# Quantized feed-forward stages: one float8 cast per block of 512 tokens in place of three

## The chip, the cores and the metric

The kernel runs on one core of one Trainium2 chip. The metric is the device time of one execution in microseconds (us); lower is better. A core has five instruction queues that matter here: TensorE (PE, matrix products, its weight loads shown apart as PEld), VectorE (DVE), ScalarE (ACT), GpSimd (POOL) and SyncE (SP, which issues the transfers).[...]

## The reference, cut to what matters

The network has four layers. The change touches the two quantized feed-forward nets in it, one in layer 2 (called f2 in the kernel) and one in layer 3 (f3). Both compute the same thing on 16,384 tokens of 96 channels, with a hidden width of 384:

```python
q_mul = lambda x: _float_quantize(x, 5, 2)     # float8, 5 exponent bits, 2 mantissa bits
q_acc = lambda x: _float_quantize(x, 5, 10)    # float16

def _qlinear(x, W, b):
    y = q_acc(jnp.einsum('bsk,nk->bsn', q_mul(x), q_mul(W)))
    return q_acc(y + q_mul(b))

h = jax.nn.relu(_qlinear(x, W1, b1))
y = _qlinear(h, W2, b2)
...
t = t + _L3_ffn_ref(_ln_t(t), L3_ffn_W1, L3_ffn_b1, L3_ffn_W2, L3_ffn_b2)
```

So each hidden value is a matrix product rounded to float16, plus a bias and again rounded to float16, cut at zero, and then rounded to float8 because it enters the second product through q_mul.

## The kernel before, in words

The token stream is kept on the chip as t, 96 channels on the partitions by 16,384 tokens, and is worked in blocks of 512 tokens (MB). A feed-forward net therefore has 32 blocks. One block goes through these steps, with the lines that the profile names:

- `center` (L881 on PE, L883 on ACT): subtract the channel mean by a product with a centring matrix, and square the result.
- `scale` (L887 on PE, L889 and L890 on ACT): sum the squares with a matrix of ones and form the reciprocal root.
- `norm` (L893 on DVE): multiply the two, and write the normed block as float8, the tile xq.
- `hidden`: three times over (m = 0, 1, 2, one third of the 384 hidden channels each) a float8 product on PE into a bank of its own (L1033), a copy to float16 on ACT (L1035, tile y), bias and cut at zero on DVE from float16 to float16 (L1037, tile y2), and a cast to float8 on POOL into a third of the tile hq (L1038).
- `project`: three products of hq with the second weights into one bank (L1044 on PE), a copy to float16 on DVE (L1046, tile z), the bias on DVE (L1048, tile z2), and the sum into t on POOL (L1050). In f3 a transfer to the output follows (L1053).

The order on every queue is the order in which the program issues the steps: the stages are built under `tc.manual_schedule`, so nothing is reordered. In `qffn` (the f3 net) iteration j of the loop issues `scale(j-1)`, `center(j)`, `norm(j-2)`, `project(j-5)`, `hidden(j-3)`. From that follows, for each queue and one iteration:

- PE: two sums of squares, two centrings, three L1044 of block j-5, three L1033 of block j-3.
- ACT: L889, L890, L883, then three L1035.
- DVE: L893 (xq), L1046 (z), L1048 (z2), then three L1037 (y2).
- POOL: one L1050 (t), then three L1038 (hq).

In `layer2` the f2 net runs with the same steps in the same order, after an attention part. Its first blocks share the loop with the last blocks of that attention: there an L978 product on PE and an L980 sum into t on DVE stand ahead of `project`, and L978 uses the same bank as L1044 (tag "o", one buffer). After those the f2 net runs alone with the norms of the next stage. Everything after f2 (the Fourier stage) starts from what f2 leaves in t, and f3 is the last stage of the kernel.

Tiles come from pools with a fixed number of buffers: y and y2 have four of 128x512 each, hq three of 128x3x512, z and z2 two, each bank of L1033 one. A writer waits until the last reader of the buffer is done. The profile drops trailing digits of names, so both y and y2 appear as y, both z and z2 as z.

Of the kernel before, what the change touches and what calls it, by code (L numbers as in the profile page):

```python
# [10 lines left out]
F16 = mybir.dt.float16  # L11
# [3 lines left out]
ALU = mybir.AluOpType  # L15
# [7 lines left out]
MB = 512  # L23
# [27 lines left out]
class Net:  # L51
# [967 lines left out]
    def ffn_steps(self, k, t, wk, psum, tags, out=None):  # L1019
        nc = self.nc  # L1020
        w1, w2, b1, b2 = self.ffn[k]
        x, hq = {}, {}

        def xq(i):
            x[i] = wk.tile([C, MB], F8, name="xq", tag="xq", bufs=2)
            return x[i]

        def hidden(i):
            xi = x.pop(i)
            q = hq[i] = wk.tile([128, 3, MB], F8, name="hq", tag="hq", bufs=3)  # L1030
            for m in range(3):
                ps = psum.tile([128, MB], F32, name="h_ps", tag=tags[m])
                nc.tensor.matmul(ps, w1[:, m * 128 : (m + 1) * 128], xi, start=True, stop=True)  # L1033
                y = wk.tile([128, MB], F16, name="y", tag="y", bufs=4)
                nc.scalar.copy(y, ps)  # L1035
                y2 = wk.tile([128, MB], F16, name="y2", tag="y2", bufs=4)
                nc.vector.tensor_scalar(y2, y, b1[:, m : m + 1], 0.0, ALU.add, ALU.max)  # L1037
                nc.gpsimd.tensor_copy(q[:, m, :], y2, saturate=False)  # L1038

        def project(i):  # L1040
            ps = psum.tile([C, MB], F32, name="y_ps", tag=tags[3])
            q = hq.pop(i)
            for m in range(3):
                nc.tensor.matmul(ps, w2[:, m, :], q[:, m], start=m == 0, stop=m == 2)  # L1044
            z = wk.tile([C, MB], F16, name="z", tag="z", bufs=2)
            nc.vector.tensor_copy(z, ps)  # L1046
            z2 = wk.tile([C, MB], F16, name="z2", tag="z2", bufs=2)
            nc.vector.tensor_scalar_add(z2, z, b2)  # L1048
            td = t[:, i * MB : (i + 1) * MB]
            nc.gpsimd.tensor_add(td, td, z2)  # L1050
            if out is not None:
                b, s = divmod(i, L // MB)
                nc.sync.dma_start(out[b, :, s * MB : (s + 1) * MB], td)  # L1053

        return hidden, project, xq

    def qffn(self, t, k, out):
# [397 lines left out]
```

## Time and profile before

| | |
|---|---|
| median of 3 runs | 4002.08 us (3991.09 to 4005.25) |
| the profiled execution | 4009.92 us |
| span of its trace, first to last instruction | 4007.8 us |
| busy in the span: PE, DVE, ACT, POOL | 3303.4, 3186.9, 2421.0, 2944.4 us |
| f2 net, first to last L1038 | from 3160.5 us, about 144 us |
| f3 net, last 125 us of the span | first L1046 at 3885.7 us, last L1038 at 4000.4 us |

Busy time is what an engine's instructions covered between their first and last moment, waiting inside an instruction included. A group line of the profile reads: line, engine, operation, output<-inputs, shape and type of output and input, count, then the busy time in us and the mean of one instruction in ns, then the idle time of the engine ahead of these instructions and what ended it. A line of the timeline reads: start in us from the span's beginning, length in us, engine, line, operation, names and shapes, how many equal instructions it joins, and in square brackets the idle time before it and what released it. Instructions on one engine overlap slightly in such lists[...].

### The profile page before, as it was taken

How to read it: one execution, taken by the hardware profiler on the slowest of the kernel's cores; microseconds unless marked ns; L12 is line 12 of the kernel's file. 1: busy time of each engine (PE TensorE's matmuls, PEld its weight loads, DVE VectorE, ACT ScalarE, POOL GpSimd, SP SyncE). 2: the span in 40 equal slices, each digit the busy share in tenths (PEclk: the TensorE clock that was granted, in tenths of full speed). 3: DMA queues.
4: the chain of work that ended last, by engine and by line, in shares of the span. 5: the costliest groups of instructions: out<-in, count | busy, mean ns of one | idle time of the engine just before them, and what ended most of it. 6: DMA issues, size and time to landing. Idle time of an engine off the chain costs nothing. (4 is left out here: it accounts for less than half of the span.)

```text
span 4007.8 us, 45514 instructions
## 1 busy us (share of the span) xinstructions
PE 3303.4 (82%) x14174; PEld 1425.1 (36%) x14174; DVE 3186.9 (80%) x2772; ACT 2421.0 (60%) x4644; POOL 2944.4 (73%) x1571
## 2 busy tenths in 40 slices
PE   6888878888888788888878888686999888998877
PEld 3222222222222222222222222186445435676642
DVE  5999999999999999999999999832652593444549
ACT  4666667667666766766666666231445575665547
POOL 2999999999999999999999999811000273444428
PEclk8888878878888888888888888667999998999989
DMA  7567566756666675666567666375000000011111
GB/s 184 137 161 174 135 160 157 175 131 168 166 154 148 162 170 138 162 166 167 141 161 169 147 155 158 82 226 178 1 0 1 1 0 6 25 35 35 42 41 54
DMA packets 183295, 468.13 MB, mean 117 GB/s; under 512 B 53240, under 2 KB 55170, under 8 KB 179972
## 3 DMA queue, kind: packets, MB, share of 16 engines
q1 hardware_dynamic: 183048, 465.21, 46.8%
q8 instruction: 113, 1.85, 0.2%
q14 instruction: 134, 1.07, 0.1%
HBM read 391.53 MB, written 73.50 MB: 116 GB/s over the span
## 5 line engine op out<-in xcount | busy, mean ns | idle before, releaser
L496 POOL TENSOR_TENSOR hs<-hs,crep 128x1024 f32<-128x1024 f32 x768 | 1796.2, 2363 | 27.2 <-DVE hs L490 22.4
L454 PE MATMUL rep<-dbl,sel_b 32*128 32x512 f32 x1152 | 409.0, 787 | 460.4 <-DVE hs L490 434.4
L474 POOL TENSOR_TENSOR up<-udb,brep 128x1024 f32<-128x1024 f32 x256 | 604.9, 2363 | 8.5 <-DMA brep<-cd 8.5
L468 ACT ACTIVATE da<-ddb,nega 128x1024 f32<-128x1024 f32 x512 | 584.9, 1149 | 14.9 <-DMA ddb<-dd 7.4
L468 ACT ACTIVATE dap<-ddb,nega 128x1024 f32<-128x1024 f32 x256 | 286.3, 1118 | 419.6 <-DVE hs L490 417.5
L515 PE MATMUL y<-hs,sel_r 128*32 128x512 f32 x3072 | 483.2, 697 | 6.1 <-POOL hs L496 6.1
L490 DVE TENSOR_TENSOR_SCAN hs<-da,state,rep 128x1024 f32<-128x1024 f32 x192 | 450.8, 2348 | 16.7
L490 DVE TENSOR_TENSOR_SCAN hs<-da,state,u 128x1024 f32<-128x1024 f32 x192 | 450.9, 2348 | 11.2 <-DVE u L486 1.4
L490 DVE TENSOR_TENSOR_SCAN hs<-dap,state,up 128x1024 f32<-128x1024 f32 x192 | 447.1, 2329 | 7.0 <-ACT dap L468 6.9
L454 PEld LDWEIGHTS rep<-dbl,sel_b 32*128 32x128 f32 x1152 | 109.6, 219 | 761.6 <-issue 510.0
L210 PE MATMUL ps<-n,w_x 97*64 97x512 f32 x1536 | 368.0, 622 | 8.1 <-ACT n L323 5.4
L486 DVE TENSOR_TENSOR u<-udb,rep 128x1024 f32<-128x1024 f32 x256 | 314.6, 1229 | 42.1 <-PE rep L454 10.9
L486 DVE TENSOR_TENSOR rep<-udb,rep 128x1024 f32<-128x1024 f32 x256 | 310.7, 1214 | 0.4
L1038 POOL CAST hq<-y 128x512 fp8e5<-128x512 f16 x192 | 118.0, 638 | 229.3 <-issue 143.0
L210 PEld LDWEIGHTS ps<-n,w_x 97*64 97x64 f32 x1536 | 109.8, 141 | 258.8 <-issue 209.2
L515 PEld LDWEIGHTS y<-hs,sel_r 128*32 128x32 f32 x3072 | 66.6, 117 | 364.5 <-issue 192.7
L382 POOL TENSOR_TENSOR du<-delta,xc 128x512 f32<-128x512 f32 x96 | 122.3, 1274 | 67.5 <-DMA gp_x<-in_x 52.1
L1177 POOL TENSOR_TENSOR av<-av,ec 128x780 f32<-128x780 f32 x32 | 58.8, 1838 | 152.3 <-ACT av L1174 152.3
L224 PE MATMUL ps<-xc,xproj 64*102 64x512 f32 x384 | 163.2, 1014 | 3.5 <-ACT xc L344 3.5
L358 ACT COPY dbl<-ps 102x512 f32<-102x512 f32 x64 | 34.3, 588 | 210.4 <-PE ps L224 210.4
L911 POOL MEMSET h<- 1x4096 f32 x1 | 3.5, 3506 | 212.9 <-DVE n L824 212.9
L490 DVE TENSOR_TENSOR_SCAN hs<-da,rep 128x1024 f32<-128x1024 f32 x64 | 146.5, 2289 | 5.4
(256 smaller groups left out, 6545.7 us busy)
## 6 DMA issues: line engine op xcount, KB each, us to landing
ddb<-dd SPq DMA_DIRECT2D x768, 128.0 KB
udb<-ud SPq DMA_DIRECT2D x768, 128.0 KB
crep<-cd SPq DMA_DIRECT2D x512, 128.0 KB
brep<-cd SPq DMA_DIRECT2D x256, 128.0 KB
dd<-delta SPq DMA_DIRECT2D x64, 384.0 KB
ud<-du SPq DMA_DIRECT2D x192, 128.0 KB
band<-in_band SPq DMA_DIRECT2D x24, 1024.0 KB
gt<-in_idft SPq DMA_DIRECT2D x64, 256.0 KB
```

Source lines behind the costliest of these rows:

```text
L210: nc.tensor.matmul(ps[rows], w[:, 64 * p : 64 * p + 64], rhs[:, at.start + shift : at.stop + shift], start=k == 0, stop=k == len(ws) - 1, ...
L224: nc.tensor.matmul(ps, w[rows, p], x[rows, p], start=start and p == 0, stop=p == 2)
L382: nc.gpsimd.tensor_mul(u, m["delta"][:, of], m["xc"][:, of])
L454: nc.tensor.matmul(x[:, at], sel_b[rows, order[t][1]], made[k]["dbl"][rows, at], start=True, stop=True)
L468: nc.scalar.activation(da, made[k]["dd", h, j], AF.Exp, scale=nega[:, col : col + 1])
L474: nc.gpsimd.tensor_mul(u, made[k]["ud", h, j], made[k]["brep", g])
L486: nc.vector.tensor_mul(u, made[k]["ud", h, j], x)
L490: nc.vector.tensor_tensor_scan(hs[:, 1:], made[k].pop(("da", t)), u, 0.0 if s == 0 else st, ALU.mult, ALU.add)
L496: nc.gpsimd.tensor_mul(hs[:, :T], hs[:, 1:], made[k]["crep", order[t][1]])
L515: nc.tensor.matmul(made[k]["y", p][row : row + 32], sel_r, made[k]["hs", t][:, at], start=False, stop=True, skip_group_check=True,)
L1038: nc.gpsimd.tensor_copy(q[:, m, :], y2, saturate=False)
L1177: nc.gpsimd.tensor_add(v[:, 2:4], v[:, 0:2], ec)
```

## The change

Inside `hidden`, the tile y2 becomes one tile of 128x3x512 with two buffers. The three L1037 write its three thirds, and after the loop one POOL instruction casts all of it (1536 elements per partition) into hq. Nothing else in the kernel changes.

```diff
             q = hq[i] = wk.tile([128, 3, MB], F8, name="hq", tag="hq", bufs=3)
+
+            y2 = wk.tile([128, 3, MB], F16, name="y2", tag="y2", bufs=2)
             for m in range(3):
                 ps = psum.tile([128, MB], F32, name="h_ps", tag=tags[m])
                 nc.tensor.matmul(ps, w1[:, m * 128 : (m + 1) * 128], xi, start=True, stop=True)
                 y = wk.tile([128, MB], F16, name="y", tag="y", bufs=4)
                 nc.scalar.copy(y, ps)
-                y2 = wk.tile([128, MB], F16, name="y2", tag="y2", bufs=4)
-                nc.vector.tensor_scalar(y2, y, b1[:, m : m + 1], 0.0, ALU.add, ALU.max)
-                nc.gpsimd.tensor_copy(q[:, m, :], y2, saturate=False)
+                nc.vector.tensor_scalar(y2[:, m], y, b1[:, m : m + 1], 0.0, ALU.add, ALU.max)
+            nc.gpsimd.tensor_copy(q, y2, saturate=False)
```

The loop of the f3 net around it, unchanged:

```python
for j in range(n + 5):
    if 0 <= j - 1 < n:
        scale(j - 1)
    if j < n:
        center(j)
    if 0 <= j - 2 < n:
        norm(j - 2, xq(j - 2), saturate=False)
    if 0 <= j - 5 < n:
        project(j - 5)
    if 0 <= j - 3 < n:
        hidden(j - 3)
```

## The prediction

> **What bounds the kernel now.** The change touches two stretches, so I read the groups of instructions of those first, then the timeline of one stretch. Groups of the f3 net (3880 to 4008 us; columns: busy us, mean ns, idle before):
>
> ```profile
> L1037 DVE TENSOR_SCALAR y<-y,f3b1q 128x512 f16<-128x512 f16 x95 | 69.8, 784 | 2.5 <-ACT y L1035 2.1
> L1038 POOL CAST hq<-y 128x512 fp8e5<-128x512 f16 x96 | 59.1, 640 | 78.6 <-DVE y L1037 78.6
> L1050 POOL TENSOR_TENSOR t<-t,z 96x512 f32<-96x512 f32 x32 | 44.7, 1397 | 17.4 <-DVE z L1048 17.4
> ```
>
> The reader is to see that L1037 is the largest group, 784 ns on average with hardly any idle time before it. DVE looks full (98.95 of the 100 us from 3886 to 3986). The timeline of DVE and then of POOL over two blocks shows what it is full of:
>
> ```profile
> 3936.41 0.35 DVE L1048 TENSOR_SCALAR z<-z,f3b2q 96x512 f16<-96x512 f16 x1
> 3936.68 0.87 DVE L1037 TENSOR_SCALAR y<-y,f3b1q 128x512 f16<-128x512 f16 x3
> 3937.47 0.68 DVE L893 TENSOR_TENSOR xq<-xc_ps,rs 96x512 fp8e5<-96x512 f32 x1
> 3938.07 0.67 DVE L1046 CAST z<-y_ps 96x512 f16<-96x512 f32 x1
> 3938.78 0.50 DVE L1048 TENSOR_SCALAR z<-z,f3b2q 96x512 f16<-96x512 f16 x1
> 3939.20 3.60 DVE L1037 TENSOR_SCALAR y<-y,f3b1q 128x512 f16<-128x512 f16 x3
> ...
> 3944.03 0.35 DVE L1048 TENSOR_SCALAR z<-z,f3b2q 96x512 f16<-96x512 f16 x1
> ```
>
> ```profile
> 3936.84 1.72 POOL L1050 TENSOR_TENSOR t<-t,z 96x512 f32<-96x512 f32 x1 [0.98 <-DVE z L1048]
> 3938.50 1.86 POOL L1038 CAST hq<-y 128x512 fp8e5<-128x512 f16 x3
> 3940.33 1.15 POOL L1050 TENSOR_TENSOR t<-t,z 96x512 f32<-96x512 f32 x1
> 3941.43 1.22 POOL L1038 CAST hq<-y 128x512 fp8e5<-128x512 f16 x2
> 3942.86 0.61 POOL L1038 CAST hq<-y 128x512 fp8e5<-128x512 f16 x1 [0.21 <-DVE y L1037]
> ```
>
> The same three L1037 take 0.87 us in one block and 3.60 us in the next. In the fast block POOL is held: its L1050 shows 1.72 us there and 1.15 us in the next block. In the slow block POOL runs and DVE is held: in narrow windows its second L1037 runs from 3939.81 to 3941.63 and ends 0.15 us after POOL's L1050 (3941.48); the third is held through two casts. DVE and POOL take turns at something that only one can have. Two blocks take 7.62 us (3936.41 to 3944.03), 3.81 each. ACT needs 3.21 a block when it never waits (L889 at 3939.27, the next at 3942.48). PE needs about 3.0 (six float8 products 0.22 apart, four float32 passes 0.43 apart). Neither sets 3.81; the turns do.
>
> **What the Trainium skill says.** "SBUF — State Buffer", section "Who interferes with whom": a DVE instruction in a two-port mode and a GpSimd instruction share one port pair under an exclusive lock, held for the whole instruction, and the other one blocks. "VectorE: DVE Perf Modes", the perf-mode tier table, puts float16 `tensor_scalar` from and to SBUF, which L1037 and L1048 are, in the four-times mode that needs both ports, while an operand in PSUM (L893, L1046, L980) rules two-port modes out. The trace agrees: L893 and L1046 keep 0.67 to 0.68 us whatever POOL does, and L1037 goes from 0.34 to 1.81.
>
> **The change part by part.** POOL issues 64 casts of 1536 elements in place of 192 of 512.
>
> *The price of the long cast* is not in the trace; the nearest rows are POOL's other one-input work:
>
> ```profile
> L768 POOL COPY x<-xt 64x1024 f32<-64x1024 f32 x12 | 12.4, 1034 | 139.1 <-PE cv_ps L790 74.7 <-DVE xt L748 64.3
> L916 POOL MEMSET h<- 1x4096 f32 x2 | 7.0, 3506 | 23.7 <-PE m_ps L844 23.7
> L729 POOL MEMSET xt<- 128x768 f32 x2 | 1.5, 770 | 8.1 <-PE ps L224 8.1
> L319 POOL MEMSET n<- 97x3 f32 x8 | 0.8, 104 | 1.3 <-DVE n L143 1.3
> ```
>
> From 3 to 768 elements a memset grows by 666 ns, 0.87 ns an element, above a fixed 0.1 us; to 4096 it is 0.83. "GPSIMD Engine Reference", § 3.1, gives 1.03 cycles an element for light bodies, at its 1.2 GHz 0.86 ns, plus a dispatch per instruction. If the copy has that slope, 1034 = 1024 x 0.86 + 153; the cast at its usual 0.60 to 0.61 us gives 512 x 0.86 + 160 or so: the same law. So I take 1536 x 0.86 + 160 = 1.48 us, and 1.43 behind another POOL instruction, as a cast in a row ends 0.56 after the one before although it shows 0.61. Bounds: 1.34 if nearly all the fixed part goes, 1.68 (3 x 0.56) if nothing is fixed. I take 1.43 since two different operations fit one slope.
>
> *The order of turns.* The cast now waits for all three L1037. Behind it on POOL is queued only the next block's L1050, which needs a later z2. Let the cast of one block end at 0. The next z2 (L1048) has been waiting for the port and ends at 0.16, the handover seen above. The three L1037 follow 0.26 apart (0.87 = 0.34 + 2 x 0.26), the last ending at 0.94. L1050 is ready after z2 but, as in the fast block, gets the port 0.14 before the last L1037 ends (3938.56 - 1.15 = 3937.41 against 3937.55): from 0.80 to 1.95. The cast follows directly: 1.95 + 1.43 = 3.38. DVE, free at 0.94, does L893 and L1046 and wants the port for z2 some 1.3 us later, after L1050 has handed on, and waits for the cast; it has about 1.1 us to spare. If L1050 slips in earlier, between the L1037s, the same pieces are summed in another order.
>
> So a block takes **3.38 instead of 3.81 us**, with the port busy or changing hands throughout. What hid the waits before is gone, so I check who is next: ACT 3.21, PE 3.0. The products L1044 of a block start at 0.1 after its cast, its queue-mates L1033 0.65 later, ACT's three copies end near 2.8, and the L1037 that read them start at 3.54 (the next turn): 0.7 us of slack. The new y2 has two buffers: its first L1037 waits for the cast two blocks back, over by then. The build also puts a POOL wait on the cast (hq, three blocks back) and on z2 (the sum two blocks back): both long met, no time.
>
> *How often.* Starts of L1046 are 7.62 us per pair for 20 blocks of f2 and 24 of f3: 44 x 0.43 = 18.9 us. Two single blocks of 4.18 gain 0.8 each: 1.6.
>
> *The first f2 blocks*, with the attention's L980, have another order. Timeline of DVE:
>
> ```profile
> 3181.81 0.69 DVE L1046 CAST z<-y_ps 96x512 f16<-96x512 f32 x1 [0.94 <-PE y_ps L1044]
> 3182.53 0.35 DVE L1048 TENSOR_SCALAR z<-z,f2b2q 96x512 f16<-96x512 f16 x1
> 3182.80 2.68 DVE L1037 TENSOR_SCALAR y<-y,f2b1q 128x512 f16<-128x512 f16 x3
> 3185.40 0.67 DVE L893 TENSOR_TENSOR xq<-xc_ps,rs 96x512 fp8e5<-96x512 f32 x1
> ```
>
> DVE, L980, L1044 and L1046 form one serial chain of 5.86 us. The second L1037 waits for L1050 and stays so. The third ends at 3185.48 only because casts of its own block take the port; with the cast behind all three it ends 0.26 after the second (3184.31), 0.9 us earlier. The long cast then runs beside L893 and L980, which need no port. Six such blocks: 5.4 us. Three more of 6.5 us stand in stretches where PE runs at half clock and has the late step (L978): nothing.
>
> Sum: 18.9 + 1.6 + 5.4 = 26 us. Nothing later takes it back: POOL, ACT and DVE go in order into the Fourier stage, and f3 is the end. The ends of the two nets I count at nothing: only the last cast is waited for at its full length, 0.9 us more than a short one. Against the profiled execution, 4009.92 - 26 = 3984; that execution was 8 us above the median, so 4002.08 - 26 = **3976 us**.
>
> **The rivals.**
> - *Nothing is fixed in a cast* (1.68): 3.63 a block; 44 x 0.18 + 1.1 + 5.4 = 14, so 3988. For it: L496 and L1050, two-input work, scale with size almost without a fixed part. Against: the memsets and the copy.
> - *Another engine binds.* ACT (3.21) and PE (3.0) are close, and the whole hq now comes at once, so L1044 and L1033 bunch. If that holds a block at 3.7: 44 x 0.11 + 1 + 5.4 = 11, so 3991. Against: the 0.7 us of slack.
> - *Better:* the cast is 1.3 or less and ACT's 3.21 binds: 44 x 0.60 + 7 = 33, so 3969.
> - *Slower:* one cast costs more than three. It decides from 1.86 us in the row (1.21 ns an element), where a block is 3.81 again. At the 2.31 ns of POOL's two-input L496 (2363 for 1024) it is 3.55, a block 5.50, and 44 x 1.69 = 74 us are lost: 4076. Against: every one-input row.
>
> That the change does not do what it says is excluded: the built program has 64 casts of 128x1536.
>
> **How the numbers follow.** Forecast 0.60 (3976, by itself 3969 to 3983), nothing fixed 0.20, another engine 0.10, better 0.06, slower 0.04. The range 3966 to 3993 takes in the first four but the edges. A measurement here can tell about 0.5%, 20 us, from no change. Faster by more: most of the forecast (0.52), the better case and a little of "nothing fixed": 0.61. Slower: 0.04. Within: 0.35.
>
> **What would show it.** L1038 x64 near 1.48 us; the 2.37 and 5.25 us alternation replaced by even blocks near 3.4; L1037 near 0.34 with the wait moved to L1048 (about 1.5 us); the first f2 blocks near 5 us. I am wrong if the cast is over 1.7, if L1037 still takes 1 us, or if DVE shows idle time before L1037 for ACT.

## The result and the profile after

The changed kernel takes 3971.51 us (median of 5 runs, 3964.75 to 3973.91) against 4002.08 us (5 runs, 3991.09 to 4005.25). The ratio is 0.9923, 95% interval 0.991 to 0.9937: 31 us, with 25 to 36 in the interval. 3976 was forecast. Its profiled execution took 3972.29 us, 37.6 less than that of before, which was itself 8 us above its median.

The groups of the f3 net after the change (line, engine, operation, names and shapes, count, then busy us, mean ns and idle time before):

```profile
L1038 DVE TENSOR_SCALAR y<-y,f3b1q 128x512 f16<-128x512 f16 x96 | 54.9, 619 | 7.1 <-ACT y L1037 6.5
L1039 POOL CAST hq<-y 128x1536 fp8e5<-128x1536 f16 x32 | 46.9, 1467 | 89.8 <-DVE y L1038 86.9 <-PE h_ps L1035 2.3 <-PE y_ps L1045 0.6
L1051 POOL TENSOR_TENSOR t<-t,z 96x512 f32<-96x512 f32 x32 | 37.9, 1185 | 8.7 <-DVE z L1049 8.7
```

All lines of this part of the code have moved by one or two: L1038 is the old L1037, L1039 the old L1038, L1049 the old L1048, L1051 the old L1050; in the text below I keep the old numbers where both kernels are meant. "Dense blocks" are the blocks of both nets that alternated in the kernel before, and the same blocks in the others; the "first f2 blocks" are those that share the loop with the attention. The long cast takes 1.467 us, the bias-and-cut instruction 619 ns on average instead of 784, the sum 1.19 us instead of 1.40. The timeline of DVE and of POOL over one block:

```profile
3897.73 0.47 DVE L1049 TENSOR_SCALAR z<-z,f3b2q 96x512 f16<-96x512 f16 x1
3898.12 1.76 DVE L1038 TENSOR_SCALAR y<-y,f3b1q 128x512 f16<-128x512 f16 x3
```

```profile
3896.58 1.47 POOL L1039 CAST hq<-y 128x1536 fp8e5<-128x1536 f16 x1 [0.57 <-DVE y L1038]
3898.28 1.19 POOL L1051 TENSOR_TENSOR t<-t,z 96x512 f32<-96x512 f32 x1 [0.23 <-DVE z L1049]
3900.03 1.47 POOL L1039 CAST hq<-y 128x1536 fp8e5<-128x1536 f16 x1 [0.57 <-DVE y L1038]
```

The reader is to see that the blocks are alike now: the three L1037 take 1.76 us instead of 0.87 and 3.60 in turn, and a block takes 3.45 us (3896.58 to 3900.03). Of the three only the second is held, for the length of POOL's sum (in a narrow window it runs 1.24 us, from 3898.38 to 3899.62); the first and the third take 0.34.

One dense block, in the f2 net, goes another way. There the three L1037 run unheld (0.86 us, from 3267.03), POOL's sum is held until they are done, and the next z2 waits for the cast:

```profile
3267.19 1.71 POOL L1051 TENSOR_TENSOR t<-t,z 96x512 f32<-96x512 f32 x1 [0.22 <-DVE z L1049]
```

```profile
3269.20 1.26 DVE L1049 TENSOR_SCALAR z<-z,f2b2q 96x512 f16<-96x512 f16 x1
```

The first f2 blocks, DVE:

```profile
3179.74 0.35 DVE L1049 TENSOR_SCALAR z<-z,f2b2q 96x512 f16<-96x512 f16 x1
3180.01 1.77 DVE L1038 TENSOR_SCALAR y<-y,f2b1q 128x512 f16<-128x512 f16 x3
3181.70 0.68 DVE L893 TENSOR_TENSOR xq<-xc_ps,rs 96x512 fp8e5<-96x512 f32 x1
3182.30 0.73 DVE L980 SCALAR_TENSOR_TENSOR t<-o_ps,vec,t 96x512 f32<-96x512 f32 x1
3183.98 0.69 DVE L1047 CAST z<-y_ps 96x512 f16<-96x512 f32 x1 [0.94 <-PE y_ps L1045]
3184.77 0.35 DVE L1049 TENSOR_SCALAR z<-z,f2b2q 96x512 f16<-96x512 f16 x1
```

The three take 1.77 us instead of 2.68, and the serial chain, L1049 to L1049, is 5.03 us instead of 5.86. Where the time went, from the starts of L1046 (z) and the stages' first products in the two profiled executions:

| stretch | before, us | after, us | saved | forecast |
|---|---|---|---|---|
| f2, first ten z | 55.1 | 45.2 | 9.9 | 5.4 |
| f2, tenth to last z | 82.3 | 74.3 | 8.0 | 9.4 |
| Fourier stage (L1124 to L881) | 544.5 | 537.4 | 7.1 | 0 |
| f3, first L881 to first z | 22.3 | 21.0 | 1.3 | 0 |
| f3, first to last z | 116.8 | 106.1 | 10.7 | 11.1 |
| all else | 3186.8 | 3186.5 | 0.3 | 0 |

The two nets alone give 28.6 us, close to the 31 of the medians. The other rows can't be put down to the change: f3's start also takes 21.0 us in the kernel with six buffers below, whose casts are those of before, and on the Fourier stage's 7.1 us see below.

### The profile page after: what moved, and what is told of

Same layout as the page of the kernel before. It is cut to its first block, busy times and chain, and to the rows that moved or that the text cites. A ratio compares the mean times of both kernels' runs of the same rounds, so it can differ in the third digit from the quotient of the medians.

```text
span 3970.5 us, 45322 instructions
## 1 busy us (share of the span) xinstructions
PE 3291.6 (83%) x14174; PEld 1420.1 (36%) x14174; DVE 3155.9 (79%) x2772; ACT 2419.9 (61%) x4644; POOL 2912.9 (73%) x1443
## 5 line engine op out<-in xcount | busy, mean ns | idle before, releaser
L1039 POOL CAST hq<-y 128x1536 fp8e5<-128x1536 f16 x64 | 93.9, 1467 | 253.7 <-issue 144.0
```

The lines of the kernel that those rows point to most:

```text
L1039: nc.gpsimd.tensor_copy(q, y2, saturate=False)
```

## The experiments

Theory: the gain comes from turns at the port that DVE and POOL share. With three casts, POOL's casts get the port between the L1037; with the cast behind all three they don't. Rivals: size alone (POOL has 1.47 us of casts a block instead of 1.8), and room (y2 has six thirds of space instead of four). Medians stand beside those of the kernel before on the same chip: 3999.24 us for the first four, 4001.46 for the next three, 4000.61 for the last two.

**Order without size.** Three casts again, behind the three L1037, the last third first:

```diff
-            nc.gpsimd.tensor_copy(q, y2, saturate=False)
+            for m in (2, 1, 0):
+                nc.gpsimd.tensor_copy(q[:, m], y2[:, m], saturate=False)
```

> The changed kernel with three casts of 512 again, issued behind all three L1037 and the last third first, so that the first cast waits for the same moment as the long one. Order without size. Turns theory (the gain is that casts no longer get the port among the three L1037): a block is the chain of the changed kernel with 3 x 0.56 to 0.60 in place of 1.47, so 3.55 to 3.75 us, the first f2 blocks stay near 5.0, total 3980 to 3992. Rival, size alone (the gain is only POOL's work, 1.8 down to 1.47): nothing is left of it, 4002, first f2 blocks 5.86.

Measured: 3985.62 us, ratio 0.9965 (0.9953 to 0.9977), 14 us saved. Dense blocks 3.72 us, first f2 blocks 5.03. POOL's timeline:

```profile
3922.35 1.19 POOL L1052 TENSOR_TENSOR t<-t,z 96x512 f32<-96x512 f32 x1 [0.23 <-DVE z L1050]
3924.11 1.74 POOL L1040 CAST hq<-y 128x512 fp8e5<-128x512 f16 x3 [0.57 <-DVE y L1038]
```

The three casts take 1.74 us where the one takes 1.47, and the block is longer by just that 0.27 (3.72 against 3.45). So order and size are separate: order alone brings all of the gain in the first f2 blocks (45.2 us for ten, as in the changed kernel) and 0.09 us of each dense block's 0.36; size brings the other 0.27. Neither size alone nor turns alone is right for the dense blocks: with the casts behind the L1037, the 0.27 us by which the cast is shorter came off the block in full, and that was most of its gain. Over the whole kernel order alone brings 14 of the 31 us.

**Room.** The kernel before with `tag="y2", bufs=6` in place of 4.

> The kernel before with six y2 buffers of 512 in place of four, as much room as the changed kernel has; casts as before. Rival, buffers (y2's writer was waiting for room): most of the gain appears, near 3975. Turns and size theories: no change, 4002 within noise, blocks alternate 2.37 and 5.25 as before.

Measured: 4003.98 us, ratio 1.0009 (1.0002 to 1.0016), no gain. Blocks alternate 2.44 and 5.29 (2.37 and 5.25 before). Room was not what was missing.

**Is DVE free to wait?** One more copy of the PSUM bank per block:

```diff
             nc.vector.tensor_copy(z, ps)
+            extra = wk.tile([C, MB], F16, name="extra", tag="extra", bufs=2)
+            nc.vector.tensor_copy(extra, ps)
```

> The changed kernel with one more DVE instruction per block behind L1046, a second copy of the same PSUM bank to an unused float16 tile (0.67 us, no port needed). The prediction's step (DVE wants the port 1.1 us before the cast ends, so it has that to spare): blocks stay 3.45, total 3972 plus about 6 for the serial first f2 blocks. The reading of the trace after (the sum gets in after the first L1037, so z2 asks only 0.3 us before the cast ends): the block grows by 0.35, to 3.8, total near 3998.

Measured: 3990.82 us, ratio 0.9979 (0.9972 to 0.9985); dense blocks 3.74 us, first f2 blocks 5.43. DVE's timeline:

```profile
3920.64 0.67 DVE L1047 CAST z<-y_ps 96x512 f16<-96x512 f32 x1
3921.24 0.67 DVE L1049 CAST extra<-y_ps 96x512 f16<-96x512 f32 x1
3921.84 0.34 DVE L1051 TENSOR_SCALAR z<-z,f3b2q 96x512 f16<-96x512 f16 x1
```

The copy takes 0.60 us of DVE's row (3921.24 to 3921.84) and the block grows by 0.29. DVE had 0.3 us to spare, not 1.1, so the second reading was the right one, though its 3.8 us and 3998 were somewhat too much. Here z2 isn't held any more (0.34 us) and DVE is busy throughout (85.0 us of the 85 from 3875 to 3960): DVE sets the block.

**The cast on DVE.** `nc.vector.tensor_copy(q, y2, saturate=False)` in place of the GpSimd one.

> The changed kernel with the long cast on DVE; POOL keeps only the sum, 1.19 us a block. Turns theory: the port is used 1.2 us by POOL and about 2 by DVE. If the cast runs at two elements a cycle (0.86 us) and the sum runs beside L893 and L1046, a block is 3.3 and the total 3962; if the sum gets in after the first L1037 as in the changed kernel, DVE is held 0.9 us longer, 4.2 and 4015. If the cast runs at one element a cycle (1.65 us), 4.0 or more and 4005 or more.

Measured: 4032.47 us, ratio 1.0078 (1.0055 to 1.01), slower than before. The groups of its f3 net on DVE:

```profile
L1038 DVE TENSOR_SCALAR y<-y,f3b1q 128x512 f16<-128x512 f16 x96 | 55.2, 624 | 6.1 <-ACT y L1037 5.5
L1039 DVE CAST hq<-y 128x1536 fp8e5<-128x1536 f16 x32 | 31.6, 987 | 1.1
```

The cast takes 0.99 us on average on DVE (0.96 in most blocks), less than on POOL. L1037 still averages 624 ns, since POOL's sum still gets in once a block. The block is 4.37 us: what was taken off POOL was put on the engine that was nearly full. The expectation's second case, a little worse.

**The tile or the place of the casts?** One y2 tile as in the changed kernel, three casts inside the loop as before:

```diff
                 nc.vector.tensor_scalar(y2[:, m], y, b1[:, m : m + 1], 0.0, ALU.add, ALU.max)
+                nc.gpsimd.tensor_copy(q[:, m, :], y2[:, m], saturate=False)
-            nc.gpsimd.tensor_copy(q, y2, saturate=False)
```

> One y2 tile of 128x3x512 as in the changed kernel, but three casts inside the loop as before. In all kernels with the one tile so far POOL's sum got the port after the first L1037, in both kernels with separate tiles the three L1037 of the quick block kept it. If the casts' place made that difference: blocks alternate 2.37 and 5.25 as before, total 4000. If the tile (with it the waits on the L1037) made it: no alternation, the second L1037 held by the sum and the third by casts in every block, as in the first f2 blocks; even blocks of 3.8 to 4.0, first f2 blocks 5.86, total 3998 to 4010.

Measured: 3998.88 us, ratio 0.9994 (0.9985 to 1.0003). DVE's timeline:

```profile
3920.20 3.63 DVE L1038 TENSOR_SCALAR y<-y,f3b1q 128x512 f16<-128x512 f16 x3
...
3925.40 0.87 DVE L1038 TENSOR_SCALAR y<-y,f3b1q 128x512 f16<-128x512 f16 x3
```

The alternation is back. The tile and its waits bring nothing; the casts' place and number do it.

**Without any cast.** `tensor_scalar` writes float8 into `q[:, m]` itself, y2 and the cast are gone.

> The three L1037 write float8 into hq themselves and no cast is left. Changed in the computation: the sum of product and bias is rounded once, to float8, without the float16 step between. POOL keeps 1.19 us a block. If L1037 stays near 0.35 us with two ports and the sum gets in once per block: DVE needs 3.3 a block and ACT 3.2, total 3962 to 3968. If it runs at one element a cycle without the second port (0.68): 3.65 a block, total 3980 to 3985. First f2 blocks 5.0 or a little over. Rival, size of POOL's work: POOL has 1.5 us a block less again than in the changed kernel, so another 20 us or more, 3950.

Measured: 3960.4 us, ratio 0.9888 (0.9869 to 0.9907), the shortest of all, at the price of one rounding. L1037 with float8 output takes 0.48 us when it isn't held, not 0.35. Dense blocks come as 2.84, 2.9 and 3.75 in turn, 3.17 on average in f3; first f2 blocks 5.39. Two ACT lines one block apart:

```profile
3902.30 0.70 ACT L889 ACTIVATE rs<-v_ps,eps 96x512 f32<-96x512 f32 x1
3905.46 0.70 ACT L889 ACTIVATE rs<-v_ps,eps 96x512 f32<-96x512 f32 x1
```

From 3862 to 3945 us L889 starts every 3.17 us, and ACT is never idle for more than 0.03 us; PE shows no idle time at all (its ends are modelled), while DVE is idle for 2.8 of the 83 us. Taking POOL's cast of 1.47 us out of a block thus shortens a dense block by only about 0.3 more, because ACT is full then, and by the profile PE too. Of the versions that keep every rounding, the changed kernel is the fastest one tried.

**A longer POOL chain.** One more cast of 512 on POOL behind the long one, into an unused tile:

```diff
             nc.gpsimd.tensor_copy(q, y2, saturate=False)
+            extra = wk.tile([128, MB], F8, name="extra", tag="extra", bufs=2)
+            nc.gpsimd.tensor_copy(extra, y2[:, 0], saturate=False)
```

> The changed kernel with one more cast of 512 per block on POOL behind the long one, into an unused tile. If the chain cast, z2, first L1037, sum, third L1037, cast sets the dense blocks: they grow by 0.4 to 0.6 us, to 3.85 to 4.05, and the first f2 blocks (a serial chain without the cast) stay at 5.0; total about 3971 + 54 x 0.5 = 3998. If ACT or PE set them: less than 0.3 more.

Measured: 3989.09 us, ratio 0.9961 (0.9945 to 0.9976). Dense blocks 3.80 us, first f2 blocks 5.03 as before the addition. POOL's timeline:

```profile
3919.95 1.47 POOL L1039 CAST hq<-y 128x1536 fp8e5<-128x1536 f16 x1 [0.55 <-DVE y L1038]
3921.36 0.70 POOL L1041 CAST extra<-y 128x512 fp8e5<-128x512 f16 x1
3922.02 1.18 POOL L1053 TENSOR_TENSOR t<-t,z 96x512 f32<-96x512 f32 x1
```

The block grows by 0.35 us, a little less than the theory had it (0.4 to 0.6) and more than the 0.3 at most that ACT or PE would have left. The reason is in the lines: the sum starts 0.60 us after the long cast's end (3921.42 to 3922.02) where in the changed kernel it starts 0.23 after it, since the 0.23 us in which POOL waited for z2 now lie beside the second cast. That is 0.37 of the chain. That the first f2 blocks stay as they were shows that POOL's casts are not in their chain.

**Off the port.** The last pair lets L1037 read the product from its PSUM bank. By the Trainium skill, "VectorE: DVE Perf Modes", the perf-mode tier table, an operand in PSUM rules the two-port modes out. ACT's copy and the first rounding to float16 are left out, in both kernels of the pair; the edit of the one with three casts:

```diff
                 ps = psum.tile([128, MB], F32, name="h_ps", tag=tags[m])
                 nc.tensor.matmul(ps, w1[:, m * 128 : (m + 1) * 128], xi, start=True, stop=True)
-                y = wk.tile([128, MB], F16, name="y", tag="y", bufs=4)
-                nc.scalar.copy(y, ps)
...
-                nc.vector.tensor_scalar(y2, y, b1[:, m : m + 1], 0.0, ALU.add, ALU.max)
+                nc.vector.tensor_scalar(y2, ps, b1[:, m : m + 1], 0.0, ALU.add, ALU.max)
```

> The kernel before with L1037 reading the product straight from its PSUM bank; the ACT copy L1035 and with it the first rounding to float16 are left out. A PSUM operand keeps L1037 off the port it shares with POOL. Turns theory: L1037 takes 0.67 us every time, whatever POOL does; blocks no longer alternate and DVE sets them (0.60 + 0.70 + 0.27 + 3 x 0.60 = 3.4 us); and the three casts of 512 lose nothing against one: this and its twin with the one cast within 0.1 us a block, 5 us in total, both near 3968 to 3975. First f2 blocks 5.0 to 5.4 in both.

> The changed kernel with L1037 reading the product straight from its PSUM bank (L1035 and the first rounding to float16 left out). Turns theory: as its twin with three casts, 3.4 us a block, since with L1037 off the port there is nothing left for the merging to save. Rival, size alone: POOL's work is 0.33 us a block less here, so 15 to 20 us faster than the twin.

Measured: with three casts 3980.74 us, ratio 0.9945 (0.9929 to 0.9962); with one 3989.38 us, ratio 0.9972 (0.9959 to 0.9985). The groups of the f3 net, first with three casts, then with one:

```profile
L1035 DVE TENSOR_SCALAR y<-h_ps,f3b1q 128x512 f16<-128x512 f32 x96 | 65.8, 738 | 5.0 <-PE h_ps L1033 5.0
L1036 POOL CAST hq<-y 128x512 fp8e5<-128x512 f16 x96 | 55.4, 612 | 73.7 <-DVE y L1035 73.6
L1046 DVE TENSOR_SCALAR z<-z,f3b2q 96x512 f16<-96x512 f16 x32 | 11.4, 355 | 1.2
```

```profile
L1036 DVE TENSOR_SCALAR y<-h_ps,f3b1q 128x512 f16<-128x512 f32 x96 | 65.6, 733 | 2.4 <-PE h_ps L1035 2.4
L1037 POOL CAST hq<-y 128x1536 fp8e5<-128x1536 f16 x32 | 47.0, 1468 | 94.2 <-DVE y L1036 94.2
L1047 DVE TENSOR_SCALAR z<-z,f3b2q 96x512 f16<-96x512 f16 x32 | 15.2, 475 | 3.3
```

The trace agrees with that page: L1037 takes 0.73 to 0.74 us on average in both, whatever POOL does (over all 192 of the second kernel 0.729 to 0.751), and the casts of the first take 0.601 to 0.622. With L1037 off the port the same merging is a loss: blocks of 3.56 us with three casts, 3.72 with one. Two expectations failed: blocks of 3.4 us and totals of 3968 to 3975 were too short, since the L1037 follow one another 0.66 us apart and not 0.60; and the twins, expected within 0.1 us, are 0.16 apart, against the merging. The short casts follow their L1037 one by one and are done when z2 wants the port (355 ns); the long one starts only behind the last L1037 and holds z2 (475 ns). DVE sets the block here (busy 84.2 of the 85 us from 3875 to 3960 in the first, 82.5 in the second). For that reason the pair shows that L1037 and POOL no longer hold each other, but it can't judge size alone: POOL is busy with casts for 0.26 us less a block in the second kernel, and a shorter POOL has nothing to shorten where DVE sets the block.

## Why the prediction was right, point by point

*The cause.* Right. L1037 and L1048 are held by POOL and hold it; instructions with an operand in PSUM are not. The pair off the port shows it in both directions. What the gain consists of is two things that the prediction had in one chain: in the first f2 blocks the order of the turns alone, in the dense blocks mostly the shorter cast (0.27 of 0.36 us).

*The price of the long cast.* Right: 1.48 us by itself was taken, 1.467 measured; behind another POOL instruction 1.43, and 1.45 in the one block where it stands so (3268.86). Slope and fixed part from POOL's memsets and copy carried over to a cast.

*The block.* 3.38 forecast, 3.45 measured; with 44 such blocks it is 3 us. The step that failed is the order: "in the fast block, gets the port 0.14 before the last L1037 ends". In the changed kernel the sum gets it after the first L1037 instead. That order had been named as giving the same sum, and nearly does: 0.14 for z2 after the cast's end, 0.09 to the sum, 1.19, then 0.15 and 0.27 for the second and third L1037, 0.15 to the cast, 1.47, in all 3.46. The 0.07 over the forecast lies half in the cast (1.47 where 1.43 was taken) and half in the sum (1.19 where 1.15 was taken): both now start on a POOL that stands idle, not directly behind another POOL instruction. In the one block that took the forecast order, the two z2 end 3.35 us apart (3267.11 and 3270.46), close to the 3.38. Among the dense blocks the sign "the wait moved to L1048 (about 1.5 us)" is seen only there, where L1048 takes 1.26 us; in the others the wait is in the second L1037 (1.24) and L1048 takes 0.47.

*What is to spare on DVE.* With it fell "about 1.1 us to spare": the second L1037 is held for the sum, so DVE is free 0.9 us later, and the run with one more DVE copy found 0.3. It had no effect on the time, but the merged kernel is closer to the next limit than the prediction said. Two limits are about equally near: DVE with 0.3 us to spare in a block of 3.45, and ACT with 0.28, since its least is 3.17 in the kernel without a cast, close to the 3.21 of the prediction.

*The first f2 blocks.* The mechanism was right and the term too small: 5.4 forecast, 9.9 measured. The six blocks of 5.86 went to 5.03 (4.96 forecast). The three of 6.5, counted at nothing because PE ran at half clock there, went to 5.03 as well: they lost the same 0.83 us, and the half clock (a granted clock of 0.5 of full speed) is gone. Nine times 0.83 is 7.5 of the 9.9 us; by this estimate the other 2.4 are the clock's. In these blocks PE ran at half clock three times for 3.4 us, 10.2 in all, in each of the four kernels whose blocks stayed at 5.86 or more (before, six buffers, one tile, the cast on DVE), and not at all in the seven with blocks of 5.46 or less. The Trainium skill, "TensorE: Matmul & The Clock Gate", Part 1, says that the gate is set by how busy PE has lately been. That fits: from 3159.0 us to the tenth z PE was busy for 50.1 of 65.3 us, products stretched by the half clock included, and in the changed kernel for 45.1 of 55.2. But the share of a whole stretch doesn't decide it: with the extra DVE copy it is 45.3 of 59.2 us, 77% as in the kernel before, without half clock. Where the limit lies is not shown.

*The sum.* 26 us forecast, 31 in the medians. Two misses partly cancel: the dense parts of the two nets gave 18.7 us instead of 20.5, the first f2 blocks 9.9 instead of 5.4. The sum so came nearer to the nets' 28.6 us than its largest miss alone would have it.

*"Nothing later takes it back."* Right, and the Fourier stage was 7.1 us shorter in the profiled execution, where no instruction changed. In the ten other profiles that stage takes 534.1 to 540.0 us, in kernels with and without alternation; the profile before, with 544.5, stands out. PE was at half clock for 57.0 to 68.3 us of it. The two other kernels with alternating blocks lie at 538.2 and 540.0, the changed one at 537.4. Whether any of it belongs to the change was not settled: beside the nets' 28.6 us the medians leave 2 us for it, the upper end of their interval 7.

*The slower rival.* The cast at 1.467 us lies well under its point of decision at 1.86.

**Left open.** Who gets the port at a contested moment. In the quick block of before, the sum starts 0.16 us after the first L1037 and the second L1037 0.26 after it, and the sum is held until all three are done (1.72 us). In the changed kernel the same two starts stand at the same distances (3898.12, 3898.28, 3898.38), and the sum goes first (1.19). The tile was tried and isn't the reason. In the one block of the changed kernel that goes the other way, the starts again stand at the same distances (3267.03, 3267.19, 3267.29), and the sum is held (1.71). What decides is not in the starts that the trace shows.

## What to carry to other kernels

When an instruction's duration jumps between a few fixed values, look at what the other engine does in those moments before counting it as work: here an engine at 99% busy was waiting inside its instructions. Merging small instructions on one side of a shared port paid twice here, in fixed parts and in fewer interruptions of the other side, while L1037 contended for the port; with L1037 off the port the same merging made z2 wait and lost time. And before moving work to the other side of such a port, ask which engine has room: the cast was faster on DVE by itself, and the kernel slower by 0.8%.

## What the runs showed that was not expected

- The DVE cast from float16 to float8 of 128x1536 takes 0.96 us when it isn't held, and bias-and-cut with float8 output 0.48 us against 0.34 with float16 output.
- 0.83 us off a serial chain of 5.86 also ended a half-clock state of PE (10.2 us of the stretch before, none after).
- The merging changes its sign with L1037's place: 0.36 us gained per dense block with L1037 on the shared port, 0.16 us lost with L1037 reading PSUM.
- One kernel shows both orders at the port, with starts at equal distances: in one dense block of the changed kernel the three L1037 keep the port and the sum is held (1.71 us), in the others the sum goes first (1.19 us).
